# Counts of W2 into a tile of their own, and one gather later: one stage of a ternary feed-forward kernel

## The chip, the cores and the metric

The kernel runs on one core of one Trainium2 chip. A core has five engines, each with a queue of its own: TensorE (PE; its weight loads are shown as PEld), VectorE (DVE), ScalarE (ACT), GpSimd (POOL) and SyncE (SP), which here only starts transfers. They wait for each other by semaphores. TensorE writes to PSUM; VectorE and ScalarE read PSUM and SBUF; GpSimd works on SBUF and issues the gathers and the output's transfers. The metric is the device time of one execution in microseconds (us), as the median over runs. Times below that are given as a point ("at 73.93") count from the start of the profiled execution.

## The reference

```python
w = weights[conditions]                       # (128, 64, 64), one matrix for each batch entry
c = jnp.einsum('bct,bcd->bdt', x, w)          # x: (128, 64, 512) f32

def ternarize(W, threshold):                  # threshold 0.05
    absW = jnp.abs(W)
    delta = threshold * jnp.max(absW)
    mask = absW > delta
    n = jnp.maximum(jnp.sum(mask), 1)
    alpha = jnp.sum(jnp.where(mask, absW, 0.0)) / n
    return alpha * jnp.sign(W) * mask

h = gelu(c @ ternarize(W1).T + b1)            # W1: (2048, 512)
y = h @ ternarize(W2).T + b2                  # W2: (512, 2048)
scale = jnp.max(jnp.abs(y)) / 7 + 1e-8
out = x + jnp.clip(jnp.round(y / scale), -7, 7) * scale
```

Each weight becomes -1, 0 or 1 times one factor alpha. For W2 the factor needs two totals over the whole matrix: the number of weights over the threshold, and the sum of their magnitudes.

## The kernel before

The 8192 token rows (128 batch entries of 64) are worked through in 16 blocks of 512. One block is four pairs of batch entries, of 128 rows each. In each block a pair is mixed with its gathered matrices (the tile `pc`, in PSUM, four products by `mix`), and the result is split into a high part, copied by ScalarE (`act.copy`), and a low part, the difference, by VectorE (`condition`, `split`; the tiles `x0` and `x1`, in the profile both called `x`). Layer 1 makes 16 chunks of 128 hidden features (`ph`, eight products each, of high and low parts), ScalarE applies gelu, and hidden values are split again into high and low parts (`h`). Layer 2 adds up four tiles `py` over the 16 chunks, 8 products per chunk (`layer2`). Blocks 2 to 12 use a variant of layer 1 with fewer products; it isn't touched. At the end the largest |y| is found, y is quantized and added to x, and the output goes out.

The weights as signs (-1, 0, 1) are made once, in block 0, beside its products. W1 and W2 are each four quarters ("groups") of 128 x 2048. For W1, `mask1` makes masks in the tiles `masks`, `signed1` multiplies them with signs into `terns`, and TensorE counts the masks (`count1`, the tile `number`). For W2, `signed2` takes two VectorE instructions per group: a comparison into a half of the tile `junk`, and a second one that makes the group's signs in `terns2`. Then three things are made of each group of `terns2`:

- `count2` (line 526): ScalarE squares the signs and adds them up; the squares themselves are not needed and go to `junk[:, g % 2]`
- `kept` (line 639): ScalarE copies the signs into `w2t`, in float8, for the later blocks (the same copies for W1 go to `w1t`)
- `sum2` (line 531): VectorE multiplies the signs with W2's group `nat2[g]` and adds up, one instruction and one that reads the accumulator

GpSimd widens signs into the form that TensorE reads (`widen1`, `widen2`: the tile `wf`), chunk by chunk, and issues the gathers of the pairs' matrices (`fetch`, the tile `wg`), four for each block; it places them in `diag` (`place`) for `mix`.

Order: every engine's instructions run in the order in which the Python code records them (the class `InOrder`), so a line that stands earlier in the code runs earlier on its engine. A tile that is written again makes its writer wait for the readers of what stood there. The pool `big` has 20 slots of 8 KB a partition which tiles take over from each other; the pool `ps_c`, which holds `pc`, has two buffers.

Two places are touched. At the start of block 0 (lines 556 to 562) the gathers of block 1 stand round the first two widenings:

```python
fetched += [fetch(1, j) for j in range(3)]
widen1(0, 0)
widen1(0, 1)
fetched += [fetch(1, 3)]
```

In block 0's layer 2 (lines 643 to 668) one pass of the loop is a chunk `hc`, 0 to 13. `signed2(2)` is recorded in pass 0 and `signed2(3)` in pass 3. Passes 4, 6, 8, 10 count a group, passes 5, 7, 9, 11 copy it to float8; passes 5, 7, 9, 11 also mix and split a pair of block 1 (`condition(1, j, ...)`) and then call `sum2(j)`. Block 1's first layer 1 chunk follows (line 856); its products need the high and low parts of all four pairs. `alpha_2` (line 543) adds up counts and sums and is called in block 1 after two chunks.

Of the kernel before, what the change touches and what calls it, by code (L numbers as in the profile page):

```python
# [35 lines left out]
AF = mybir.ActivationFunctionType  # L36
# [22 lines left out]
def tile_cond_ternary_ffn(  # L59
# [20 lines left out]
    PAIRS = 4  # L80
    BLK = PAIRS * P
    NB = B // (2 * PAIRS)
    NG = 4
# [101 lines left out]
    def fetch(n, j):  # L185

        pair = n * PAIRS + j
        wg = gather.tile([P, D], F32, tag="wg", name=f"wg_{pair}")
        pool.indirect_dma_start(
            out=wg[:, :],  # L190
            out_offset=None,
            in_=table,
            in_offset=bass.IndirectOffsetOnAxis(ap=rows[:, pair : pair + 1], axis=0),
        )
        return wg
# [5 lines left out]
    def parts(n):  # L201
        return [big.tile([P, NT, BLK], F32R, tag="big", name=f"x{k}_{n}") for k in range(2)]
# [6 lines left out]
    def pair_of(xt, j):  # L209
        return xt[j // 2][:, j % 2, :]  # L210
# [12 lines left out]
    def condition(n, j, xp, two):  # L223
        pc = ps_c.tile([P, NT, P], F32, tag="pc", name=f"pc_{n}_{j}")
        mix(xp, j, pc)
        split(pc, *(t[:, :, j * P : (j + 1) * P] for t in two))
# [30 lines left out]
    def flat(w):  # L257
        return w.rearrange("p a b -> p (a b)")
# [3 lines left out]
    masks = [big.tile([P, 2, WCH], BF16, tag="big", name=f"masks_{i}") for i in range(2)]  # L262
    terns = [big.tile([P, 2, WCH], BF16, tag="big", name=f"terns_{i}") for i in range(2)]
    junk = big.tile([P, 2, WCH], BF16, tag="big", name="junk")
# [4 lines left out]
    def group1(tiles, g):  # L269
        return tiles[g // 2][:, g % 2, :]  # L270
# [33 lines left out]
    fetched = [fetch(0, j) for j in range(PAIRS)]  # L304
# [13 lines left out]
    def lo0(j):  # L318
        part = slice(j * P, (j + 1) * P)
        dve.tensor_tensor(  # L320
            two_next[1][:, :, part], pcs[j], two_next[0][:, :, part], ALU.subtract
        )
# [15 lines left out]
    def signed1(g, part=slice(0, WCH)):  # L338
        dve.tensor_tensor(
            group1(terns, g)[:, part],  # L340
            group1(masks, g)[:, part],
            group1(signs, g)[:, part],
            ALU.mult,
        )
# [33 lines left out]
    def widen1(n, hc):  # L378

        if n == 0:  # L380
            w = w1f[hc % 4]
            g, i = divmod(hc, GH)
            pool.tensor_copy(flat(w), group1(terns, g)[:, i * T : (i + 1) * T])
        else:
            w = w1f[hc % 2]
            pool.tensor_copy(flat(w), w1t[:, hc])
        wide1[n, hc] = w

    def widen2(n, hc):
        if n == 0 and hc < NH - LAG:  # L390
            w = w2f[hc % 4]
        elif n == NB - 1 and hc == NH - 1:

            w = flat(w1f[0])
        else:
            w = w2f[hc % 2]
        if n == 0 and hc < NH - LAG:
            g, i = divmod(hc, GH)
            pool.tensor_copy(w, group1(terns2, g)[:, i * T : (i + 1) * T])
        else:  # L400
            pool.tensor_copy(w, w2t[:, hc])
        wide2[n, hc] = w
# [29 lines left out]
    def low(n, hc):  # L432

        open_low.pop((n, hc), lambda: None)()

    def layer2(n, hc, js=range(PAIRS)):
        two = hidden[n, hc]
        w = wide2[n, hc]
        if n not in ypsum:
            ypsum[n] = [  # L440
                ps_y.tile([P, T], F32, tag=f"py{j}", name=f"py{j}_{n}") for j in range(PAIRS)
            ]
        for j in js:
            for k in range(2):
                pe.matmul(
                    out=ypsum[n][j],
                    lhsT=two[k][:, j * P : (j + 1) * P],
                    rhs=w,
                    start=(hc == 0 and k == 0),
                    stop=(hc == NH - 1 and k == 1),  # L450
                )
# [52 lines left out]
    sums2 = const.tile([P, 2, NG], F32)  # L504
    terns2 = []

    def group2(g):
        return group1(terns2, g)
# [6 lines left out]
    def signed2(g):  # L515

        delta2, minus2 = delta
        below = junk[:, g % 2, :]
        if g % 2 == 0:
            terns2.append(big.tile([P, 2, WCH], BF16, tag="big", name=f"terns2_{g}"))  # L520
        dve.tensor_scalar(below, flat(nat2[g]), minus2, None, ALU.is_lt)
        dve.scalar_tensor_tensor(
            group2(g), flat(nat2[g]), delta2, below, ALU.is_gt, ALU.subtract
        )

    def count2(g):
        act.activation(
            junk[:, g % 2, :], group2(g), AF.Square, accum_out=sums2[:, 1, g : g + 1]
        )

    def sum2(g):
        dve.tensor_tensor_reduce(
            out=flat(nat2[g]),
            in0=flat(nat2[g]),
            in1=group2(g),
            scale=1.0,
            scalar=0.0,
            op0=ALU.mult,
            op1=ALU.add,
            accum_out=sums2[:, 0, g : g + 1],  # L540
        )
# [14 lines left out]

    mask1(0, parts1[0])
    signed1(0, parts1[0])
    fetched += [fetch(1, j) for j in range(3)]
    widen1(0, 0)  # L560
    widen1(0, 1)
    fetched += [fetch(1, 3)]
    lo0(0)
    lo0(1)
    hi0(2)
# [73 lines left out]
    def kept(t, g, tiles):  # L639

        act.copy(flat(t[:, g * GH : (g + 1) * GH]), group1(tiles, g), saturate=False)

    for hc in range(NH - LAG):
        if hc + 2 < NH - LAG:
            widen2(0, hc + 2)
        layer2(0, hc)
        if hc == 0:
            signed2(2)
        if hc == 1:
            for i in range(10, NH):  # L650
                low(0, i)
        if hc < NG:
            kept(w1t, hc, terns)
        if hc == 3:
            signed2(3)
        if hc == 4:
            two_next = parts(1)
            w2t = big.tile([P, NH, T], F8, tag="big", name="w2t")
        if 4 <= hc < 4 + 2 * NG:
            g = (hc - 4) // 2  # L660
            if hc % 2 == 0:
                count2(g)
            else:
                kept(w2t, g, terns2)
        if hc in (5, 7, 9, 11):
            j = (hc - 5) // 2
            condition(1, j, pair_of(x_next, j), two_next)
            sum2(j)
    cond[1] = two_next
    x_next, two_next, fetched = [], [], []  # L670
    hf = ring[:2]
# [281 lines left out]
    while s < len(steps):  # L953
        n, hc = steps[s]
# [116 lines left out]
```

## Time and profile before

| | |
|---|---|
| median of 3 runs | 1064.39 us (1062.46 to 1064.63) |
| profiled execution, as timed | 1062.89 us |
| its span, first to last instruction | 1061.0 us |
| busy: TensorE, its weight loads | 986.1 us (93%), 864.0 us (81%) |
| busy: VectorE, ScalarE, GpSimd | 610.9, 611.4, 628.2 us (58%, 58%, 59%) |
| mean granted clock of TensorE | 0.969 |

The span divides into a first part (to about 20 us) in which weights are loaded and thresholds found, block 0 with the making of signs (to about 85 us), fifteen more blocks (to about 988 us), and a tail in which TensorE has nothing to do and y is quantized and written. TensorE's granted clock was 1.00 in every 25 us stretch up to 975 us, and 0.50 in the tail.

How to read the lines: a line of the timeline has the start, the length, the engine, the line of code (a helper records every instruction, so it is always L55), the operation, the tiles it writes and reads, the sizes, and how many such instructions follow each other; in brackets stands how long the engine was idle before and who released it. Starts and lengths of consecutive TensorE products overlap, so the pitch from one start to the next is what a product costs.

### The profile page before, as it was taken

What the parts mean: (1) busy time and instruction counts of PE and PEld (TensorE: products, weight loads), DVE (VectorE), ACT (ScalarE), POOL (GpSimd) and SP (SyncE); (2) the same over time, 40 slices, a digit from 0 to 9 for tenths busy, and PEclk for the clock granted to TensorE, in tenths of its full rate; (3) what the DMA queues carried; (4) which work ended last, traced back from release to release, by engine and by line L of the source; (5) the groups of instructions that cost most, each with busy time, mean ns of one, the idle gap of its engine ahead of it and who ended that gap; (6) DMA issues with size and microseconds to landing.
All of it is one profiled execution on the core that took longest, in us unless ns stands there. A gap on an engine that the chain in (4) does not pass through costs nothing.

```text
span 1061.0 us, 16715 instructions
## 1 busy us (share of the span) xinstructions
PE 986.1 (93%) x5760; PEld 864.0 (81%) x5761; DVE 610.9 (58%) x1078; ACT 611.4 (58%) x1040; POOL 628.2 (59%) x1016
## 2 busy tenths in 40 slices
PE   8999999999999999999999999999999999999400
PEld 5887889999999999999999999999998888888300
DVE  7896645666656565666656565666645224232682
ACT  7974445666666565656666565656655433343481
POOL 6855656676766667676766767676664435333242
PEclk9999999999999999999999999999999999999755
DMA  9100000101000010101000010100001010041899
GB/s 361 57 20 3 23 22 12 34 6 31 15 22 23 14 32 7 39 6 32 15 22 23 14 32 5 40 6 30 16 22 43 3 40 6 1 149 33 301 413 372
DMA packets 26611, 62.20 MB, mean 59 GB/s; under 512 B 3488, under 2 KB 3488, under 8 KB 25760
## 3 DMA queue, kind: packets, MB, share of 16 engines
q1 hardware_dynamic: 19872, 42.25, 12.0%
q0 software_dynamic: 6656, 18.88, 4.6%
q8 instruction: 47, 0.77, 0.3%
q14 instruction: 36, 0.29, 0.1%
HBM read 44.34 MB, written 16.78 MB: 58 GB/s over the span
## 4 chain that ended last, share of the span: by engine, by line
PE 87%; DVE 4%; DMA 3%; ACT 2%; issue 1%; POOL 1%; SPq 1%; POOLq 0%; DVEq 0%; ACTq 0%
PE py L55 42%; PE xy L55 16%; PE ph L55 13%; PE z L55 12%; PE pc L55 5%; DMA xt<-in_x 3%; DVE h L55 1%; DVE y L55 1%; ACT diag L55 1%; DVE terns L55 1%; POOL wg L55 1%; ACT junk L55 1%; SPq L55 1%; DVE junk L55 1%; DMA wg<-in_L_cond_weights,rows 1%
## 5 line engine op out<-in xcount | busy, mean ns | idle before, releaser
L55 PE MATMUL py<-wf,h 128*128 128x512 f32 x2048 | 531.2, 395 | 0.9 <-ACT h L55 0.7
L55 PEld LDWEIGHTS py<-wf,h 128*128 128x128 f32 x2048 | 365.4, 189 | 65.1 <-DVE y L55 2.0
L55 DVE TENSOR_TENSOR h<-ring,h 128x512 fp32r<-128x512 f32 x252 | 194.7, 775 | 182.1 <-ACT h L55 182.1
L55 POOL CAST wf<-w2t 128x512 fp32r<-128x512 fp8e4 x242 | 173.7, 718 | 154.4 <-PE py L55 142.4
L55 ACT ACTIVATE ring<-ring,b1t,alpha_w 128x512 f32<-128x512 f32 x176 | 144.3, 820 | 97.7 <-DVE ring L55 97.7
L55 POOL CAST wf<-w1s 128x256 fp32r<-128x256 fp8e4 (+1 forms) x264 | 134.4, 514 | 108.9 <-PE xy L55 80.5
L55 POOL CAST wf<-w1t 128x256 fp32r<-128x256 fp8e4 (+1 forms) x240 | 156.7, 658 | 56.7 <-PE ph L55 45.2
L55 ACT CAST h<-ring 128x512 fp32r<-128x512 f32 x256 | 158.9, 621 | 8.3
L55 PE MATMUL ph<-x,wf 128*128 128x512 f32 (+1 forms) x648 | 157.6, 388 | 2.8 <-ACT x L55 2.1
L55 PEld LDWEIGHTS ph<-x,wf 128*128 128x128 f32 x648 | 119.8, 188 | 28.8 <-issue 2.5
L55 ACT ACTIVATE ring<-ph,b1t,alpha_w 128x512 f32<-128x512 f32 x80 | 62.3, 779 | 139.6 <-PE ph L55 139.5
L55 DVE TENSOR_TENSOR ring<-xy,ring 128x256 f32<-128x256 f32 (+1 forms) x176 | 97.3, 553 | 64.2 <-PE xy L55 64.2
L55 PEld LDWEIGHTS xy<-xt,wf 128*128 128x128 f32 x704 | 107.6, 189 | 14.1
L55 PE MATMUL xy<-xb,wf 128*128 128x256 f32 x704 | 112.4, 281 | 0.0
L55 PE MATMUL xy<-xt,wf 128*128 128x256 f32 x704 | 111.8, 282 | 0.0
L55 PEld LDWEIGHTS xy<-xb,wf 128*128 128x128 f32 x704 | 102.2, 190 | 7.9
L55 ACT COPY ring<-xy 128x256 f32<-128x256 f32 x176 | 65.1, 370 | 67.7 <-PE xy L55 67.7
L55 PE MATMUL z<-xt,wf 128*128 128x256 f32 x704 | 98.3, 282 | 0.0
L55 ACT COPY ring<-z 128x512 f32<-128x512 f32 x88 | 51.7, 588 | 73.9 <-DVE h L55 72.5
L55 PEld LDWEIGHTS z<-xt,wf 128*128 128x128 f32 x704 | 90.2, 190 | 0.0
L55 DVE TENSOR_TENSOR xt<-x_quarters,xt 128x512 fp32r<-128x512 f32 x44 | 33.8, 768 | 91.1 <-ACT xt L55 91.1
L55 POOL DMA_INDIRECT wg<-in_L_cond_weights,rows x64 | 73.5, 1148 | 11.7 <-issue 4.4
(103 smaller groups left out, 851.4 us busy)
## 6 DMA issues: line engine op xcount, KB each, us to landing
xt<-in_x SPq DMA_DIRECT2D x36, 512.0 KB, 7.2
out<-y POOLq DMA_DIRECT2D x30, 512.0 KB, 12.9
x_quarters<-in_x SPq DMA_DIRECT2D x48, 256.0 KB, 2.6
nat<-in_L_ffn_W SPq DMA_DIRECT2D x6, 1024.0 KB, 10.2
nat<-in_L_ffn_W SPq DMA_DIRECT2D x3, 512.0 KB, 9.0
wg<-in_L_cond_weights,rows POOLq DMA_INDIRECT x64, 2.7
w1t<-in_x SPq DMA_DIRECT2D x4, 256.0 KB, 2.6
w2t<-in_x SPq DMA_DIRECT2D x4, 256.0 KB, 2.6
```

The costliest lines, as they stand in the source:

```text
L55: return lambda *args, **kw: self._tc.keep_in_program_order(make(*args, **kw))
```

## The change

```diff
     def count2(g):
         act.activation(
-            junk[:, g % 2, :], group2(g), AF.Square, accum_out=sums2[:, 1, g : g + 1]
+            group1(masks, 2 + g % 2), group2(g), AF.Square, accum_out=sums2[:, 1, g : g + 1]
         )
...
     mask1(0, parts1[0])
     signed1(0, parts1[0])
-    fetched += [fetch(1, j) for j in range(3)]
+    fetched += [fetch(1, j) for j in range(2)]
     widen1(0, 0)
     widen1(0, 1)
-    fetched += [fetch(1, 3)]
+    fetched += [fetch(1, j) for j in range(2, PAIRS)]
...
         if hc == 4:
             two_next = parts(1)
             w2t = big.tile([P, NH, T], F8, tag="big", name="w2t")
-        if 4 <= hc < 4 + 2 * NG:
-            g = (hc - 4) // 2
-            if hc % 2 == 0:
-                count2(g)
-            else:
-                kept(w2t, g, terns2)
+        if hc in (4, 6, 8, 9):
+            g = {4: 0, 6: 1, 8: 2, 9: 3}[hc]
+            count2(g)
+            kept(w2t, g, terns2)
+            sum2(g)
         if hc in (5, 7, 9, 11):
             j = (hc - 5) // 2
             condition(1, j, pair_of(x_next, j), two_next)
-            sum2(j)
```

The squares of `count2` go to the second of the two `masks` tiles (`group1(masks, 2)` and `group1(masks, 3)`), whose masks have been used by then, instead of to `junk`. For each group count, float8 copy and sum now stand together, in passes 4, 6, 8 and 9, ahead of the `condition` of a later pass; in pass 9 they stand ahead of that pass's own `condition`. The number of instructions is the same on every engine. On ScalarE the order by groups and pairs becomes: count, copy 0; x 0; count, copy 1; x 1; count, copy 2; count, copy 3; x 2; x 3. On VectorE it was low part 0, sum 0, low part 1, sum 1, low part 2, sum 2, low part 3, sum 3, and becomes sum 0, low part 0, sum 1, low part 1, sum 2, sum 3, low part 2, low part 3. On GpSimd one gather, the third of block 1's four, moves behind the first two widenings. `masks` is used longer and `junk` less long, so that later tiles of the pool `big` take other slots than before.

## The prediction

> **What bounds the kernel now.** I read the page first: its shares of busy time and its chain of waits. The chain gives TensorE 87% of the span, so only time at which TensorE stands still, or is held, can be won.
>
> ```profile
> PE 87%; DVE 4%; DMA 3%; ACT 2%; issue 1%; POOL 1%; SPq 1%; POOLq 0%; DVEq 0%; ACTq 0%
> ```
>
> The list of what TensorE waited for is short. Two of its lines lie where the change is: 2.1 us and 0.2 us ahead of a `ph` product (the first of block 1), and 0.6 us ahead of another (the first of block 0).
>
> ```profile
> PE ph L55 <- ACT x L55: 2.1, 1, 2.1
> PE ph L55 <- POOL wf L55: 0.6, 1, 0.6
> PE ph L55 <- DVE x L55: 0.2, 1, 0.2
> ```
>
> Then the timeline by engine round these two places (start, length, engine, operation). Block 0's start, on GpSimd and TensorE:
>
> ```profile
> 16.27 0.98 POOL L55 DMA_INDIRECT wg<-in_L_cond_weights,rows  x1 [0.27 <-POOL diag L55]
> 17.55 1.11 POOL L55 DMA_INDIRECT wg<-in_L_cond_weights,rows  x1 [0.30 <-issue]
> 18.97 0.95 POOL L55 DMA_INDIRECT wg<-in_L_cond_weights,rows  x1 [0.30 <-issue]
> 19.96 1.17 POOL L55 CAST wf<-terns 128x512 fp32r<-128x512 bf16 x2
> 20.63 4.01 PE L55 MATMUL ph<-x,wf 128*128 128x256 f32 x24 [0.57 <-POOL wf L55]
> 27.23 2.79 PE L55 MATMUL number<-masks,ones_b 128*128 128x256 bf16 x24
> ```
>
> Here a third gather stands between VectorE's first signs (ready at 17.88 + 0.69 = 18.57) and the first widening. And the end of block 0's layer 2:
>
> ```profile
> 69.85 2.60 DVE L55 SCALAR_TENSOR_TENSOR terns<-nat,delta_w,junk 128x2048 bf16<-128x2048 f32 x1
> 72.38 0.68 DVE L55 TENSOR_TENSOR x<-pc,x 128x512 fp32r<-128x512 f32 x1
> 72.49 1.91 ACT L55 ACTIVATE junk<-terns 128x2048 bf16<-128x2048 bf16 x1 [4.77 <-DVE terns L55]
> 72.98 2.39 DVE L55 CUSTOM_DVE_ANT_0 nat<-nat,terns 128x2048 f32<-128x2048 f32 x1
> 73.93 1.05 PE L55 MATMUL pc<-diag,xt 128*128 128x128 f32 x8
> 77.40 2.28 DVE L55 CUSTOM_DVE_ANT_0 nat<-nat,terns 128x2048 f32<-128x2048 f32 x1
> 79.27 3.88 PE L55 MATMUL py<-wf,h 128*128 128x512 f32 x16
> 85.15 0.69 DVE L55 TENSOR_TENSOR x<-pc,x 128x512 fp32r<-128x512 f32 x1 [1.28 <-ACT x L55]
> 85.87 2.68 POOL L55 CAST wf<-w2t 128x512 fp32r<-128x512 fp8e4 x1
> 85.89 1.89 PE L55 MATMUL ph<-x,wf 128*128 128x512 f32 x7 [0.16 <-DVE x L55]
> ```
>
> The second count on ScalarE stood 4.77 us, until VectorE had the last quarter of W2's signs (72.45), because both write `junk`. From there ScalarE runs count, copy, x without a pause to 85.1 and VectorE's last low part ends at 85.84; TensorE had emptied its queue at 79.27 + 16 x 0.233 = 83.00. Block 1's second product starts at 85.89; without a wait it would be 83.00 + 0.23 = 83.23. The gap is worth 2.66 us, the largest single hole between 21 us and the tail.
>
> [...] each gather holds GpSimd 0.95 to 1.11 us. [...] a cast that takes 0.62 us alone takes 2.68 us beside a sum, which took 2.31 instead of 2.28. [...]
>
> **Part 1, the gathers.** The diff moves one gather, not two: three stood ahead of the first widening, two stand there now. After the second gather (17.55 + 1.11 = 18.66) the first cast can start at 18.70, against 19.96: 1.26 us earlier. Both queues: GpSimd then issues the third and fourth gathers at about 20.0 to 22.3; its next cast started at 22.86 for VectorE's sake, after 0.61 us idle, so that cast doesn't move, and the fourth gather ends where it did. TensorE gains less than 1.26. Its mixing ends at 20.06 and VectorE's second low part at 18.56 + 0.62 + 0.69 = 19.87, so the first product starts at 19.92, 0.71 earlier. The second half of the tokens needs the last low part, which ends at 20.72 + 0.69 = 21.41 in both. Its second product stood at 20.86 + 8 x 0.12 = 21.80 and can start at 21.45: 0.35 is left. Next, the counting products: the seventeenth of 24, at 27.23 + 16 x 0.11 = 28.99, reads the mask that VectorE ends at 27.02 + 1.63 = 28.65, so it can't be before 28.70. **0.29 us** is left. The product `total`, at 31.25, needs ScalarE's last sum (30.68 + 0.19 = 30.87), a limit of 0.32, not reached. From 31.4 to 72 us TensorE or work chained to it sets the pace, so 0.29 travels on. Bounds: 0 (another wait for VectorE that the view doesn't show) to 0.32; I take 0.29.
>
> **Part 2, the counts.** In before's clock (part 1 shifts all of it).
>
> ScalarE: its four W1 copies end at 55.52 + 7.30 = 62.82. The counts wait only for their own quarters of signs, so it never stands for `junk` again. With the pitches of the trace (count 1.91, copy 1.79, x 0.48): count 0 62.82, copy 64.73, x 66.52, count 1 67.0, copy 68.9, x 70.7 (its products end at 70.45), counts and copies 2 and 3 from 71.2 to 78.6. The 4.77 and 0.61 us are gone, and ScalarE is about 6 us early.
>
> VectorE is what comes late instead. The sums that read W2 are now recorded with the counts: sum 0 ahead of low part 0, sum 1 ahead of low part 1, sums 2 and 3 both ahead of low parts 2 and 3. Sum 0 doesn't start earlier, since VectorE works without a pause to 72.38 on signs and low parts of the hidden layer. So: sum 0 72.38 to 74.78 (2.40 with its accumulator read, from 72.98 to 75.38), low part 0 ends at 74.78 + 0.69 = 75.47; sum 1 from 75.39 for 2.29 to 77.68; low part 1 (pitch 0.61) to 78.29; sum 2 to 80.58, sum 3 to 82.87; low part 2 from 82.87, low part 3 from 83.48 to 84.17. Before it ended at 85.84.
>
> TensorE: `pc` has two buffers, and the third mixing, at 73.93, waits until low part 0 has read the first. Before, that was over at 73.06 and cost nothing. Now it is 75.47, plus 0.05 as in other handovers (85.84 to 85.89): 75.52. TensorE stands **1.59 us**, with the 16 products of chunks 10 and 11, the fourth mixing and the 16 of chunks 12 and 13 queued behind it. The fourth needs low part 1 (78.29), and TensorE is there at 78.47 + 1.59 = 80.06: no second stop. TensorE is free at 83.00 + 1.59 = 84.59, and the second product of block 1 can start at 84.82; low part 3 (84.17) is there 0.6 us earlier. ScalarE's x 3 follows the fourth mixing, 81.1 to 81.7, also in time. So 2.66 us of waiting become 1.59: **1.07 us** gained.
>
> Costs at nothing: the counts' new place is a mask tile that VectorE last read at 41.95 and TensorE at 30.0. The big tiles take other slots afterwards; the waits this makes are for work long done (W2's third quarter of signs for block 0's last layer 1 product, at 54, needed at 60.83). The cast from `w2t` at 84.75 comes earlier; it isn't on the path. If the small overlaps of casts with sums delay VectorE, there is 0.6 us of cover ahead of block 1, but none at the third mixing. Sum 0's length there is between 2.28 and 2.6[...]: 1.5 to 1.8 us of stop.
>
> Behind block 1's start, all follows TensorE: `total` at 91.26, the four results at 94.38, then 900 us of products, then the tail, whose loads wait for results. I carry the gain through whole.
>
> Sum: 0.29 + 1.07 = 1.36 us. On the profiled execution (span 1061.0, 1062.89 as timed) that is a span of 1059.6; on the median of 1064.39, 1063.0. The three timed runs spread over 2.17 us, more than the gain. I take 0.2% (2.1 us) as what a measurement can tell from no change.
>
> **Rivals.** (a) The gather is hidden anyway: part 1 gives 0, part 2 gives 1.07, so 1063.3. For it: VectorE's masks come last in that stage. Against it: TensorE shows no pause from 20.63 to 31.4, so an earlier start must show somewhere. (b) The third mixing isn't held, because VectorE reaches low part 0 in time: all 2.66 + 0.29 = 2.95 us, 1061.4, faster. Against it: the order of the instructions puts the sum first, and VectorE had no pause before 72.38. For it: six low parts at 63.33 took 4.93, 0.82 each against 0.61, so that up to 1.3 us could be won if GpSimd's casts fell otherwise. (c) Slower: [...] Four low parts at 55.86 took 3.73 us, 0.93 each, half as much again as 0.61. The same on four sums is 4 x 1.15 = 4.6 us: low part 3 at 88.8, block 1's second product at 88.8 + 0.05 - 0.29 = 88.6, 2.7 us after before's, and 1067.1. It decides from 2.0 us on (84.17 + 2.0 + 0.05 - 0.29 = 85.9), a fifth of the sums' length. Against it: after the casts at 72.61, 74.23 and 75.79 GpSimd has nothing until the layer 2 products release a buffer[...].
>
> **How the numbers follow.** Forecast 0.64, (a) 0.12, (b) 0.15, (c) 0.09. The range reaches from (b) less half a microsecond of scatter, 1060.8, to 1065.0, a little over the slowest of the three timed runs, which no gain at all would give; only most of (c) is left out. Faster by over 0.2%: (b), and 0.10 from scatter in the forecast's favour, 0.25. Slower by over 0.2%: 0.05 of (c) and 0.03 of scatter, 0.08. Within: 0.67.
>
> **What would show it.** First cast of `wf` near 18.7, first `ph` product near 19.9, `total` near 30.96. A row of counts on ScalarE from about 62.5 without VectorE as releaser. A TensorE wait of about 1.6 us at the third `pc` of this stage, released by VectorE's x, near 75.2; TensorE's wait ahead of block 1 gone; that block's first product near 84.3. I am wrong if the third mixing starts on time, if VectorE's sums are visibly longer than 2.4, or if block 1 starts where I say and the end doesn't follow.

## The result, and the profile after

| | before | changed |
|---|---|---|
| median of 16 runs each | 1064.26 us (1062.46 to 1064.71) | 1061.64 us (1061.07 to 1062.52) |
| span of the profiled execution | 1061.0 us | 1059.5 us |
| ratio of the times | | 0.9979, 95% interval 0.9972 to 0.9986 |

The changed kernel is faster by 2.2 us by the ratio, on the edge of what the prediction called measurable; the interval lies wholly below 1. The median lies 1.4 us below the forecast of 1063.0, inside the range that was stated. The two profiled executions differ by only 1.5 us, near the 1.36 us of the forecast. So two questions are left: whether the sum was right for its reasons, and where the other part of the measured gain comes from.

First what TensorE waited for in the changed kernel (total us, times, longest). The 2.1 us and the 0.6 us shown of before are gone, and a wait at a mixing has come:

```profile
PE pc L55 <- DVE x L55: 1.2, 1, 1.2
PE py L55 <- ACT h L55: 0.7, 1, 0.7
PE ph L55 <- DVE x L55: 0.3, 1, 0.3
```

The timeline of the changed kernel at block 0's start:

```profile
16.04 3.75 PE L55 MATMUL pc<-diag,xt 128*128 128x128 f32 x32
17.47 1.01 POOL L55 DMA_INDIRECT wg<-in_L_cond_weights,rows  x1 [0.30 <-issue]
18.53 1.17 POOL L55 CAST wf<-terns 128x512 fp32r<-128x512 bf16 x2
19.54 1.32 PE L55 MATMUL ph<-x,wf 128*128 128x256 f32 x9
21.19 2.94 PE L55 MATMUL ph<-x,wf 128*128 128x256 f32 x15 [0.33 <-DVE x L55]
30.75 0.28 PE L55 MATMUL total<-sums,ones_f 128*128 128x4 f32 x2
```

The same two points of the kernel before:

```profile
16.32 3.75 PE L55 MATMUL pc<-diag,xt 128*128 128x128 f32 x32
31.25 0.28 PE L55 MATMUL total<-sums,ones_f 128*128 128x4 f32 x2
```

All of this execution stands 0.28 us earlier from the start, ahead of anything that the change touches: the mixing began at 16.04 instead of 16.32. So points are compared by their distance from the mixing. `total` came 14.71 us after it here (30.75 - 16.04) and 14.93 us after it before (31.25 - 16.32). So part 1 is worth 0.22 us in this pair.

The first product starts 0.81 us earlier (3.50 us after the mixing instead of 4.31) and then waits at the tenth for VectorE's last low part, as the prediction had it. At the tenth product 0.33 us is left (21.19 - 16.04 against 21.80 - 16.32). The product behind the wait follows after 0.22 us instead of 0.12, and 0.24 us is left at the first counting products (23.97 - 16.04 against 24.49 - 16.32). The mask that the prediction took for the last limit ends at 28.42 and the seventeenth counting product starts at 28.47, at the pitch that it had before: the mask took nothing more here.

The changed kernel at the end of block 0's layer 2:

```profile
66.41 1.91 ACT L55 ACTIVATE masks<-terns 128x2048 bf16<-128x2048 bf16 x1
71.88 2.28 DVE L55 CUSTOM_DVE_ANT_0 nat<-nat,terns 128x2048 f32<-128x2048 f32 x1
74.09 0.68 DVE L55 TENSOR_TENSOR x<-pc,x 128x512 fp32r<-128x512 f32 x1
74.69 2.64 DVE L55 CUSTOM_DVE_ANT_0 nat<-nat,terns 128x2048 f32<-128x2048 f32 x1
74.82 1.16 PE L55 MATMUL pc<-diag,xt 128*128 128x128 f32 x8 [1.23 <-DVE x L55]
82.29 1.28 DVE L55 TENSOR_TENSOR x<-pc,x 128x512 fp32r<-128x512 f32 x2
84.03 1.98 PE L55 MATMUL ph<-x,wf 128*128 128x512 f32 x8
89.47 0.28 PE L55 MATMUL total<-sums,ones_f 128*128 128x8 f32 x2
```

And TensorE in the kernel before, at block 1's first product and second `total`:

```profile
85.26 0.47 PE L55 MATMUL ph<-x,wf 128*128 128x512 f32 x1 [2.10 <-ACT x L55]
91.26 0.28 PE L55 MATMUL total<-sums,ones_f 128*128 128x8 f32 x2
```

The second count runs at 66.41 without a wait for VectorE. Sum 0 stands ahead of low part 0, and the third mixing waits for that low part, as forecast: it starts 44.07 us after the first `total` (74.82 - 30.75); before it was 42.68 (73.93 - 31.25), so the stop costs 1.39 us. Block 1's eight products then run without a gap. The second `total`, a fixed way into block 1, comes 58.72 us after the first (89.47 - 30.75) instead of 60.01 (91.26 - 31.25): part 2 is worth 1.29 us here.

### The profile page after: what moved, and what is told of

Read it like the earlier page. It is cut to its first block, busy times and chain, and to the rows that moved or that the text cites. A ratio compares the mean times of both kernels' runs of the same rounds, so it can differ in the third digit from the quotient of the medians.

```text
span 1059.5 us, 16719 instructions
## 1 busy us (share of the span) xinstructions
PE 986.9 (93%) x5760; PEld 864.2 (82%) x5761; DVE 609.5 (58%) x1078; ACT 611.3 (58%) x1040; POOL 627.2 (59%) x1016
## 4 chain that ended last, share of the span: by engine, by line
PE 90%; DVE 4%; DMA 3%; ACT 1%; issue 1%; SPq 1%; POOL 0%; POOLq 0%; DVEq 0%; ACTq 0%
PE py L55 42%; PE xy L55 16%; PE ph L55 13%; PE z L55 12%; PE pc L55 5%; DMA xt<-in_x 3%; PE idle L55 1%; DVE h L55 1%; DVE y L55 1%; ACT diag L55 1%; DVE junk L55 1%; SPq L55 1%; DVE terns L55 0%; PE number L55 0%; DVE ymax L55 0%
## 5 line engine op out<-in xcount | busy, mean ns | idle before, releaser
L55 POOL CAST wf<-w1s 128x256 fp32r<-128x256 fp8e4 (+1 forms) x264 | 132.1, 505 | 110.6 <-PE xy L55 80.5
```

The costliest lines, as they stand in the source:

```text
L55: return lambda *args, **kw: self._tc.keep_in_program_order(make(*args, **kw))
```

## The experiments

**A copy of the kernel before.** The times of the kernel before lie in two groups, 5 of 16 at 1062.46 to 1063.04 and 11 at 1064.17 to 1064.71, with nothing between; those of the changed kernel don't. They are called the lower and the upper group below. The profiled execution that the prediction rests on (1062.89) is of the lower group. So the kernel before ran once more, unchanged.

> The kernel before once more, as a control: ratio 1.000 within 0.0007. It lists the span of each execution: if the two groups of times are one event of the chip's loads at the start, spans fall near 1061.0 and near 1062.6; in a profile of the upper group the gathers of block 0 would land, and the first cast of wf start, about 1.6 us later than 19.96. Rival: spans agree, and the groups come from outside the span.

Measured: ratio 0.9997 (0.9989 to 1.0006), 13 runs, six at 1063.0 to 1063.5 and seven at 1064.5 to 1065.8. Their spans form the same groups, 1061.1 to 1061.6 and 1062.5 to 1063.9. The profile caught the upper group, with a span of 1063.0. Block 0's first cast of `wf` stood at 20.05, 0.09 us later than before and not 1.6, so the gathers' landing is not the cause. Of the 2.0 us between the two spans (1063.0 and 1061.0) 1.60 come in at one place: from block 1's first product to the second `total` it is 7.60 us here (93.16 - 85.56) and was 6.00 (91.26 - 85.26). Here is TensorE ahead of block 1 in that copy, from its timeline:

```profile
85.56 0.47 PE L55 MATMUL ph<-x,wf 128*128 128x512 f32 x1 [2.10 <-ACT x L55]
86.20 3.00 PE L55 MATMUL ph<-x,wf 128*128 128x512 f32 x7 [0.16 <-DVE x L55]
88.99 2.51 PE L55 MATMUL py<-wf,h 128*128 128x512 f32 x8
```

The wait is the same 2.10 and 0.16 us as before, but the seven products behind it take 3.00 us where they took 1.89. Stretches of 1 us of the same copy (length; TensorE busy and products; granted clock, as a share of full speed; share and GB/s of transfers):

```profile
86.00:87.00 1.00, 0.84 (x4) 0.83 0.00 0
87.00:88.00 1.00, 1.00 (x4) 0.50 0.00 0
88.00:89.00 1.00, 1.00 (x4) 0.50 0.00 0
89.00:90.00 1.00, 1.00 (x4) 0.50 0.00 0
90.00:91.00 1.00, 1.00 (x6) 0.96 0.00 0
```

And the same from the first profile of the kernel before:

```profile
87.00:88.00 1.00, 1.00 (x6) 1.00 0.00 0
88.00:89.00 1.00, 1.00 (x7) 1.00 0.00 0
```

After the wait TensorE's granted clock falls to half for some 3.4 us (from the clocks shown, 0.17 / 0.5 + 3 + 0.04 / 0.5). Ahead of it TensorE was idle for 2.10 us, did one product and was idle for 0.16 us more, 3.1 us from the last `py` start (79.58 + 15 x 0.233 = 83.08) to 86.20. In the first profile the same 2.10 and 0.16 us were followed by a clock of 1.00. By the times 11 of the first 16 executions and 7 of these 13 were of the upper group. Among the executions of the same kernel that were timed beside the later experiments it was 25 of 37, 47 of 60 and 22 of 25. What decides in which executions the clock falls, no run here shows.

The mean granted clock of each execution is on record for 135 executions of the kernel before. It was 0.9693 on average in the 34 with spans up to 1061.8 us (0.969 to 0.971) and 0.9680 in the 101 with spans from 1061.9 us (0.967 to 0.969), so the longer executions have the lower clock on average, not only the one that was profiled. (An estimate from the slow stretch: 3.4 us at half the clock lower the mean over 1062 us by 0.0016.)

**The wait filled.** If the halved clock is the cause, and if it comes from TensorE standing idle (an assumption that this run tries), products that compute nothing should remove the upper group without removing the wait.

```diff
     hf = ring[:2]
+    busy = ps_h.tile([P, T], F32, tag="ph", name="busy")
+    for _ in range(18):
+        pe.matmul(out=busy[:, :P], lhsT=ones_b, rhs=ones_b, start=True, stop=True)
     widen1(1, 0)
```

> The kernel before, with 18 products of the ones tile with itself (a PSUM tile that nobody reads) in TensorE's wait ahead of block 1; all else as before. Theory of the clock ([...] 1.6 us of time each): the wait for ScalarE's x 3 stays, but it is filled; the executions near 1064.7 are gone, the median is 1063.0 to 1063.4, spans 61.0 to 61.6 over 1000, ratio 0.9988. Rival (the two groups have another cause): still two groups, ratio 1.000.

Measured: 1062.94 us, ratio 0.9989 (0.9983 to 0.9996); 20 of 21 runs lie from 1062.4 to 1063.5 and one at 1064.18. The kernel's own work is not earlier, as its timeline shows:

```profile
83.10 1.18 PE L55 MATMUL busy<-ones_b 128*128 128x128 bf16 x18
85.36 0.47 PE L55 MATMUL ph<-x,wf 128*128 128x512 f32 x1 [1.08 <-ACT x L55]
85.99 1.89 PE L55 MATMUL ph<-x,wf 128*128 128x512 f32 x7 [0.16 <-DVE x L55]
```

Block 1 starts where it did (85.36 against 85.26), its seven products take 1.89 us again, and the 1.2 us of the ratio are won by nothing else than work in the gap. The mean clock of the 21 executions is 0.969 to 0.971; that of the one at 1064.18 is 0.970, so its length has another cause, which stays open. So the upper group goes when the wait is filled. With the clock of 0.50 behind the wait in the profile and the lower mean clock of the longer executions (0.9680 against 0.9693), that puts the upper group down to the halved clock behind this wait.

**Each part alone.** First the gather with the counts as before, then the counts with three gathers ahead as before.

```diff
-    fetched += [fetch(1, j) for j in range(3)]
+    fetched += [fetch(1, j) for j in range(2)]
     widen1(0, 0)
     widen1(0, 1)
-    fetched += [fetch(1, 3)]
+    fetched += [fetch(1, j) for j in range(2, PAIRS)]
```

> Only the gather moves; counts, copies and sums stand as before. Forecast's theory: the product total comes 0.2 to 0.3 us earlier against the mixing's start, the third mixing isn't held, the wait of 2.1 us ahead of block 1 stays; span about 0.3 us shorter, ratio 0.9997. Rival (the scatter of the kernel before, with executions near 1062.8 and others near 1064.3, comes from the first gathers' landing, which only a GpSimd that is late passes on): the median falls by 1 us or more and the executions draw together, ratio 0.9985 to 0.9990.

Measured: 1064.02 us, ratio 0.9994 (0.9986 to 1.0002); still two groups (five runs to 1063.3, eight from 1064.0), since the wait of 2.1 us ahead of block 1 is still in its trace. The time alone doesn't show the gather's worth, as the interval reaches over 1; the distance from mixing to `total` does, below. The rival falls.

> Only the counts, copies and sums change; three gathers stand ahead of the first widening as before. Forecast's theory: the wait ahead of block 1 goes, the third mixing is held 1.2 to 1.4 us, block 1 starts 1.2 to 1.3 us earlier against block 0's start; ratio 0.9988. Rival (scatter from the gathers): executions keep two groups 1 to 1.6 us apart, as in the kernel before. Rival (sums delayed by casts): no gain.

Measured: 1062.21 us, ratio 0.9983 (0.9976 to 0.9991), and no two groups: 17 runs from 1061.87 to 1063.16. The third mixing waits 1.2 us in its list of waits. From `total` to block 1's second `total` the time fell by 1.3 us, as in the changed kernel. So the rival that foresaw two groups falls with the one before it, and so does the one that foresaw no gain.

From the first mixing to `total` the profiles of all kernels without added GpSimd work (the later ones among them) agree by kind: 14.93 to 15.13 us in the five with three gathers ahead of the first cast, 14.69 to 14.71 in the five with two. Part 1 is worth 0.2 to 0.4 us.

**The tile without the new order.** The prediction's stop at the third mixing comes from the sums that were moved. If so, the counts' new tile is all that is needed. One kernel takes the tile and the gather, with counts, copies and sums where they were:

```diff
-            junk[:, g % 2, :], group2(g), AF.Square, accum_out=sums2[:, 1, g : g + 1]
+            group1(masks, 2 + g % 2), group2(g), AF.Square, accum_out=sums2[:, 1, g : g + 1]
```

> The counts write to the masks tile and the gather moves, but counts, copies and sums stay where they were recorded. Forecast's theory: what is won comes from the tile alone, and the new order costs the stop at the third mixing; here ScalarE doesn't wait for junk, low part 0 is over before the third mixing, neither stop is there: span 1.3 to 1.4 us shorter than the changed kernel's, about 1058.1. Rival (the earlier places of the float8 copies are needed, as ScalarE would be late with x 2 and x 3): block 1 waits, no better than the changed kernel.

Measured: span 1058.1 us, 1060.42 us, ratio 0.9962 (0.9948 to 0.9975), the lowest ratio of all. Its five spans, 1058.1 to 1058.7, lie below all sixteen of the changed kernel, 1059.2 to 1060.6, and below all seventeen of the new order with the tile that were timed beside it (the counts alone, above), 1060.0 to 1061.1. And the tile alone, without the gather:

> The kernel before with one edit: the counts write to the masks tile. Gathers, counts, copies and sums stand as before. Theory: no stop at the third mixing, none ahead of block 1, no fall of the clock; from tile_gather's 1058.1 less what the gather brings, 0.25 to 0.45: span 1058.4 to 1058.6, ratio 0.9965. Rival (the gather is what makes tile_gather better than the changed kernel): 1059.5 or more.

Measured: span 1058.2 us, 1060.36 us, ratio 0.9966 (0.9954 to 0.9979); six spans from 1058.2 to 1059.4. The gather's few tenths don't show between the times of these two. In the trace the second `total` comes 57.18 us after the first, 2.83 us sooner than before: that is what the tile alone brings. The timeline of the kernel with the tile alone:

```profile
72.40 0.68 DVE L55 TENSOR_TENSOR x<-pc,x 128x512 fp32r<-128x512 f32 x1
73.95 1.05 PE L55 MATMUL pc<-diag,xt 128*128 128x128 f32 x8
81.31 0.68 DVE L55 TENSOR_TENSOR x<-pc,x 128x512 fp32r<-128x512 f32 x1
83.02 1.98 PE L55 MATMUL ph<-x,wf 128*128 128x512 f32 x8
```

Low part 0 is over at 73.08, the third mixing isn't held, and low part 3 (to 81.99) is there a microsecond before TensorE comes to block 1. ScalarE, though its copies stand later in the code, is early enough.

**The new order without the tile.** `junk` is written again, with the changed order.

> The changed kernel, but the counts write to junk again, in the new order. Theory (the tile of its own and the order of the sums are two changes with opposite signs): ScalarE stands again until VectorE's last signs at about 72, copies 1 to 3 then hold x 2 and x 3, low part 3 ends near 85.4 instead of 83.6; the third mixing is held as in the changed kernel and block 1 waits besides, about 1.2 us: span 1060.7. Rival (the order alone brings the gain, the tile nothing): span 1059.5.

Measured: span 1060.7 us, 1062.9 us, ratio 0.9985 (0.9978 to 0.9992). The stop at the third mixing and waits ahead of block 1, of 0.57 and 0.27 us, all stand in its timeline:

```profile
72.53 1.91 ACT L55 ACTIVATE junk<-terns 128x2048 bf16<-128x2048 bf16 x1 [4.79 <-DVE terns L55]
75.37 1.16 PE L55 MATMUL pc<-diag,xt 128*128 128x128 f32 x8 [1.23 <-DVE x L55]
84.71 1.29 DVE L55 TENSOR_TENSOR x<-pc,x 128x512 fp32r<-128x512 f32 x2 [1.81 <-ACT x L55]
85.31 0.47 PE L55 MATMUL ph<-x,wf 128*128 128x512 f32 x1 [0.57 <-ACT x L55]
86.05 1.88 PE L55 MATMUL ph<-x,wf 128*128 128x512 f32 x7 [0.27 <-DVE x L55]
```

Block 1's first product starts 54.02 us after `total` (85.31 - 31.29), in the kernel before 54.01 (85.26 - 31.25): the waiting is not less, it has been cut into two shorter waits. Its runs lie at 1062.4 to 1064.2, two of 20 above 1064. Part 1 is 0.2 to 0.4 of the 1.6 us of its ratio. For the rest the waits are no shorter, but the clock doesn't seem to fall: the mean clock of the 20 executions is 0.9698 on average, no lower than the lower group's 0.9693, and that of the two above 1064 is 0.970. So about 1.2 us are left to the clock alone, as much as the filled wait brought.

**The stop made longer.** Sums 0 and 1 both ahead of low part 0, in the changed kernel.

```diff
-            sum2(g)
+            for i in {0: (0, 1), 1: (), 2: (2,), 3: (3,)}[g]:
+                sum2(i)
```

> The changed kernel with sums 0 and 1 both ahead of low part 0. The third mixing then waits for two sums: the stop grows by one sum's pitch of 2.2 us, from 1.4 to 3.6 us. Theory of VectorE's queue: 2.2 us slower from this alone, span 1061.7. With the theory of the clock on top: the granted clock falls after the stop in nearly every execution, 1.6 us more, span 1063.3. Rival (the third mixing isn't held by low part 0): same as the changed kernel.

Measured: span 1065.1 us, 1066.86 us, ratio 1.0024 (1.0017 to 1.0031), slower than before, and 1.8 us above the expected span:

```profile
72.75 5.13 POOL L55 CAST wf<-terns 128x512 fp32r<-128x512 bf16 x2 [2.30 <-DVE terns L55]
74.73 2.68 DVE L55 CUSTOM_DVE_ANT_0 nat<-nat,terns 128x2048 f32<-128x2048 f32 x1
78.08 2.08 PE L55 MATMUL pc<-diag,xt 128*128 128x128 f32 x8 [3.84 <-DVE x L55]
79.80 5.78 PE L55 MATMUL py<-wf,h 128*128 128x512 f32 x16
```

The third mixing comes 46.70 us after `total`, 2.63 us later than in the changed kernel; the second sum took 2.68 us beside the casts, which took 5.13 for two. And 16 products of layer 2 take 5.78 us instead of 3.89. From the third mixing to the fourth, with no wait between, it is 7.34 us (85.42 - 78.08) instead of 4.68 in the changed kernel (79.50 - 74.82): 2.66 us more, where the gap ahead of block 1 was followed by 1.60 us more. An estimate by the ratio there (3.4 us at half the clock for those 1.60) is a slow stretch of 5.7 us. The mean clock of this execution is 0.967, that of the changed kernel's 0.969. The profile caught one of the longer executions: of 20 spans ten lie at 1063.5 to 1064.2, near the expected 1063.3, and ten at 1064.5 to 1065.7, so the 2.66 us are shown for this one only. No run is below 1065.5, against 1062.52 for the slowest of the changed kernel.

**GpSimd made later.** If GpSimd's queue is what the gather's move relieves, a GpSimd that is later should take the gain back. Two GpSimd memsets stand ahead of the first widening, in the kernel before and in the changed one.

```diff
+    for i in (2, 3):
+        pool.memset(flat(w1f[i]).bitcast(F32), 0.0)
     widen1(0, 0)
     widen1(0, 1)
```

> The kernel before with two GpSimd memsets of 128 x 512 (about 0.5 us each) ahead of the first widening. Theory of GpSimd's queue (three gathers put its first cast on the path): the first cast starts near 20.9 instead of 19.96, and the product total and the span come 0.6 to 1.0 us later. Rival (VectorE's masks and ScalarE's sums set the time of total anyway): less than 0.2 us.

> The changed kernel with the same two memsets. With one gather fewer ahead, the first cast starts near 19.5 instead of 18.53 and ends before the mixing is followed by layer 1; total moves less than 0.3 us, span 1059.4 to 1059.9. Rival (GpSimd is on the path in the changed kernel too): 0.6 to 1.0 us later, span 1060.3.

Measured: 1065.07 us, ratio 1.0004 (0.9996 to 1.0013), and 1062.26 us, ratio 0.9981 (0.9973 to 0.9989), span 1059.9. From mixing to `total` it is 15.45 us in the first (0.3 to 0.5 more than without memsets) and 15.13 in the second (0.42 more). Both forecasts of `total` missed: less than the 0.6 to 1.0 foreseen in the kernel before, more than the 0.3 in the changed one, whose span is still at the edge of what was foreseen. (The profile of the first caught the upper group again, with a span of 1063.4 us and a mean clock of 0.968.) The timeline of the changed kernel with memsets shows why the slack isn't there:

```profile
22.34 1.62 POOL L55 DMA_INDIRECT wg<-in_L_cond_weights,rows  x1 [0.30 <-issue]
22.56 1.28 DVE L55 TENSOR_SCALAR masks<-nat,delta_w 128x2048 bf16<-128x2048 f32 x1
23.87 2.35 DVE L55 TENSOR_TENSOR terns<-masks,signs 128x2048 bf16<-128x2048 bf16 x1
```

The last gather, now beside VectorE's mask, takes 1.62 us instead of 0.96, and VectorE's next signs 2.35 instead of 1.51, with GpSimd's casts beside them. Here two casts took 1.17 us; in the changed kernel three took 4.71 us beside the same signs, so there the casts paid. The mask that the counting products need is late: they wait 0.15 us for it, at 29.03. Here VectorE and GpSimd set the pace together; neither theory holds as written.

## Why the prediction was right, and where not

- **Part 1**: right. One gather moves, the first product starts early, and VectorE's last low part takes most of it back. Forecast 0.29 us, measured 0.2 to 0.4. In the profiled pair what was lost behind the low part was one longer step of TensorE (0.22 us instead of 0.12 to the next product), not the wait for a mask that the sum names.
- **Part 2, the stop**: right in place and releaser. Forecast 1.59 us, measured 1.39. The term that was mis-sized is sum 0 with its accumulator read: 2.40 us in the sum, but the next instruction starts 2.21 us after it (71.88 to 74.09): here the sum is 2.28 us long instead of 2.39, and the read of its accumulator overlaps its end. By block 1's first product the stop has grown to 1.54 us (53.28 us after `total`, 51.74 with the tile alone). The part as a whole was put at 1.07 us and measured at 1.29. One sign of being wrong did show: sum 1 took 2.64 us, longer than the 2.4 that was named, beside casts. It decided nothing, as block 1 waits for no low part.
- **The wait ahead of block 1**: right that it goes, wrong on its worth. "The gap is worth 2.66 us" is the wait alone; the tile alone won 2.8. In the executions of the upper group it costs 1.6 us more, in a halved clock behind it. One profiled execution without that fall stood for all, and the spread of 2.17 us in the three timed runs was taken for scatter, when it was two groups. By the means of the 16 runs: lower group 1062.76, upper 1064.42, changed kernel 1061.71. The lower group is 1.05 us slower than the changed kernel; 11/16 of 1.66 us adds 1.14; together 2.19 us, which is the ratio. So about half of the measured gain has the forecast's cause, and half is the clock, for which the sum has no term. That the median fell inside the range all the same is owed to the room that the range left for rival (b), not to the sum.
- **"I carry the gain through whole"**: nearly. TensorE is 1.8 us ahead in block 1 and 1.5 at the end. Nearly all of the loss is 0.27 us at one product group near 756 us, in all four kernels with the new order and the new tile, and in none with either alone. Its cause stays open.
- **Rivals**: (a) falls, since the gather shows. (b) falls for the changed kernel, although its 1061.4 is nearer to the median than the forecast: the third mixing is held. But it is what the tile alone does: the stop was of the new order, not of the change's purpose. (c), sums made longer by casts, didn't decide here, but in the kernel with two sums ahead a sum took 2.68 us beside the casts, against 2.28 for the one ahead of it.
- **The chances**: "within 0.2%" was held likeliest; the ratio came out just beyond it, on the faster side.

## What to carry to other kernels

A wait of TensorE can cost more than itself, in some executions and not in others (here 2.3 us of idle time, and 1.6 us more). Here two groups of times were the sign of it, and the profile showed which group it was of by the granted clock in the stretch behind the wait (0.50 or 1.00). A tile of its own for an unused output can free an engine by itself (here it alone brought 2.83 us): try it before work is moved, since what is moved ahead on an engine's queue stands in front of what others wait for (here sums ahead of the low part that frees a PSUM buffer, and a stop of 1.39 us).

## What the runs showed of the hardware

- A gap of 3.1 us with one product in it (2.10 and 0.16 us idle) was followed by half of TensorE's clock, 0.50, for 3.4 us in one profile and by a clock of 1.00 in another. By the times it was followed by the longer execution in 11 of 16 and 7 of 13 executions and in 94 of 122 others.
- The stop of 1.4 us in the changed kernel, 1.23 us of it idle, was followed by a clock of 1.00 in its profile (each stretch from 74 to 82 us), and no mean clock of its 16 executions, nor of the 17 with the counts alone, is below 0.969.
- With 18 products of 0.07 us in the gap, none of 21 executions has a mean clock below 0.969.
- Behind the stop in which TensorE was idle for 3.84 us, 24 products took 7.34 us instead of 4.68 in the one profile of it.
- Where a sum of VectorE and a cast of GpSimd ran beside each other, a cast took 2.68 us instead of 0.62 in one place, beside a sum of 2.31 (before), and a sum 2.64 instead of 2.28 in another, beside casts (the changed kernel).
